# A Mamba scan: the softplus correction shared out between two engines, and a sixth half buffer for the states

## The chip, the cores and the metric

The kernel runs on one core of one Trainium2 chip. A core has five engines that work side by side and meet only through semaphores: TensorE (PE in the profile, with its weight loads as PEld), VectorE (DVE), ScalarE (ACT), GpSimd (POOL) and SyncE (SP), which here only starts transfers. Everything is computed in fp32. The metric is the device time of one execution in microseconds (us), from the first to the last instruction of the core.

## What is computed

The network has four layers on an image batch of 2 x 256 x 32 x 32: two Mamba blocks in a row (layer 0), a dilated 7 x 7 convolution attention (layer 1), a linear attention and a mixture of experts (layer 2), a softmax attention and another mixture of experts (layer 3). The change touches layer 0 alone. Cut to what matters, one Mamba block on a sequence `u` of 1024 positions is

```python
xs, res = split(u @ in_w + in_b)                  # 512 channels each
xs = silu(causal_conv4(xs) + conv_b)
dt, Bm, Cm = split(xs @ xproj_w)                  # 16 + 16 + 16
delta = softplus(dt @ dt_w + dt_b)
dA  = exp(delta[..., None] * A)                   # 16 states per channel
dBu = delta[..., None] * Bm[:, :, None, :] * xs[..., None]
# for each position t:  h = dA_t * h + dBu_t ;  y_t = sum over states of h * C_t
y = (ys + xs * Dp) * silu(res)
out = y @ out_w + out_b                           # then layernorm, added to u
```

The softplus is computed as max(z, 0) + log(1 + e), with e = exp(-|z|). When e is small, 1 + e is rounded, so the kernel adds what the rounding lost: e - ((1 + e) - 1). This term is the softplus correction.

## The kernel before: the parts that matter

The 2 x 1024 positions are cut into 4 chunks of 512 per block, so two blocks make 8 chunks, and a tile holds 128 channels on the partitions. There are 4 such groups of channels (NDC) and 16 states (NS). Each chunk has a `front` (projection, convolution, softplus), a `scan` and a `back` (gate, output projection, layernorm). The first front runs alone, with VectorE doing its softplus; the seven others run beside the scan of the chunk before, with GpSimd doing it. A Python generator cuts each part into pieces, and every slot of a scan (16 states x 4 channel groups = 64 slots) takes a piece of what is to run beside it:

```python
before = m.scan(j, before, chain(*done, *(a.front(k) for a, k in ahead), islice(aside, 7)))
done = [m.back(j)]
```

The framework's scheduler then settles the order of the instructions on each engine; that order need not be the order of the source.

The end of `front`, the softplus (L340 to L369; `eng` is GpSimd unless the front runs alone):

```python
for dc in range(NDC):
    # ... ps = dt_w.T @ dt, on TensorE
    nc.scalar.activation(e[:, dc, :], ps, AF.Abs, bias=b)                       # L349
    # ...
        nc.scalar.activation(delta[:, dc, :], ps, AF.Relu, bias=b)              # L353
    yield
parts = [slice(dc, dc + 1) for dc in range(NDC)] if alone else [slice(0, NDC)]
for a in parts:
    nc.scalar.activation(e[:, a, :], e[:, a, :], AF.Exp, scale=-1.0)            # L357
for a in parts:
    nc.scalar.activation(ln[:, a, :], e[:, a, :], AF.Ln, bias=net.one)          # L359
yield
for dc in range(NDC):
    eng.tensor_scalar(du[:, dc, :], e[:, dc, :], 1.0, -1.0, ALU.add, ALU.add)   # L362
    eng.tensor_sub(du[:, dc, :], e[:, dc, :], du[:, dc, :])                     # L363
    yield
    eng.tensor_add(ln[:, dc, :], ln[:, dc, :], du[:, dc, :])                    # L365
    eng.tensor_add(delta[:, dc, :], delta[:, dc, :], ln[:, dc, :])              # L366
    eng.tensor_mul(du[:, dc, :], delta[:, dc, :], xs[:, dc, :])                 # L367
    yield
```

The scan. Per state n: GpSimd makes the input `h` = du * B in two halves of two channel groups each (one tile of 128 x 1024, five such tiles in the ring), ScalarE makes dA = exp(delta * A) into PSUM (three tiles), VectorE scans in place over `h`, TensorE transposes the scanned states of the state before, and VectorE accumulates them, weighted by C, into `ya`:

```python
for n in range(NS):
    # ... b = B of state n, broadcast over the partitions by a transfer (ring of 4)
    for g in range(NDC // G):                                      # two halves
        h = scanp.tile(half, F32, tag="h", ..., bufs=5)
        nc.gpsimd.tensor_mul(h, du[:, g * G : (g + 1) * G, :], ...b...)        # L414
    for dc in range(NDC):                                          # one slot each
        da = self.ps_da.tile([P, TC], F32, tag="da", ...)
        nc.scalar.activation(da, delta[:, dc, :], AF.Exp, scale=...)           # L421
        nc.vector.tensor_tensor_scan(h, da, h, ..., ALU.mult, ALU.add)         # L425
        next(before, None)         # a piece of rest(n - 1): transpose L393, accumulate L402
        if n or dc:
            next(between, None)    # a piece of back(j - 1), front(j + 1), aside
```

Of `back`, the last pieces: the layernorm's output is turned back, scaled into a tile `r` and added to the running sequence `xt` by GpSimd; in the second block the input image `x` is loaded and added too.

```python
r = self.one.tile([P, TC], F32, tag="r", ..., bufs=2)
nc.scalar.activation(r, ps, AF.Identity, scale=..., bias=...)
nc.gpsimd.tensor_add(xt[:, cc, tok], xt[:, cc, tok], r)
if self.x is not None:
    x = self.one.tile([P, TC], F32, tag="x", ..., bufs=2)
    nc.sync.dma_start(x, ...)
    nc.gpsimd.tensor_add(xt[:, cc, tok], xt[:, cc, tok], x)
```

`ln` and the gate of `back` share one buffer (tag "gate", one tile), and `e` shares one with the convolution's input. Beside the scans run also the pieces of `aside`, which prepare the convolution weights of layer 1 (transpose, copy to `w1ts`, multiply, copy out).

Of the kernel before, what the change touches and what calls it, by code (L numbers as in the profile page):

```python
# [9 lines left out]
F32 = mybir.dt.float32  # L10
I32 = mybir.dt.int32
BF16 = mybir.dt.bfloat16
AF = mybir.ActivationFunctionType
ALU = mybir.AluOpType
# [4 lines left out]
P = 128  # L19
# [7 lines left out]
TC = 512  # L27
# [35 lines left out]
class Net:  # L63


    def __init__(self, ctx, tc, cols, rows):
        self.tc, self.nc = tc, tc.nc
        nc = self.nc
        const = ctx.enter_context(tc.tile_pool(name="const", bufs=1))
        self.small = ctx.enter_context(tc.tile_pool(name="small", bufs=4))  # L70
        self.cols = const.tile([P, NCOLS], F32, name="cols_sb")
        nc.scalar.dma_start(self.cols, cols)
        self.rows = const.tile([P, NROWS], F32, name="rows_sb")
        self.rows_dram = rows
        self.ident = const.tile([P, P], F32, name="ident")
        make_identity(nc, self.ident)
        self.eps5 = const.tile([P, 1], F32, name="eps5")
        nc.vector.memset(self.eps5, 1e-5)
        self.eps6 = const.tile([P, 1], F32, name="eps6")
        nc.vector.memset(self.eps6, 1e-6)  # L80
        self.one = const.tile([P, 1], F32, name="one")
        nc.vector.memset(self.one, 1.0)
        self.ones_row = const.tile([1, P], F32, name="ones_row")
        nc.vector.memset(self.ones_row, 1.0)

# [125 lines left out]
class Mamba:  # L211
# [46 lines left out]
    def front(self, j, alone=False):  # L258


        net, nc, m, one, two = self.net, self.net.nc, self.m, self.one, self.two
        eng = nc.vector if alone else nc.gpsimd
# [3 lines left out]
        xs = two.tile([P, NDC, TC], F32, tag="xs", name=f"{m}_xs_{j}")  # L266
# [71 lines left out]
        delta = two.tile([P, NDC, TC], F32, tag="delta", name=f"{m}_delta_{j}")  # L338
        e = one.tile([P, NDC, 3 + TC], F32, tag="pre", name=f"{m}_e_{j}")[:, :, :TC]
        ln = one.tile([P, NDC, TC], F32, tag="gate", name=f"{m}_ln_{j}")  # L340
        du = two.tile([P, NDC, TC], F32, tag="du", name=f"{m}_du_{j}")
# [13 lines left out]
        parts = [slice(dc, dc + 1) for dc in range(NDC)] if alone else [slice(0, NDC)]  # L355
        for a in parts:
            nc.scalar.activation(e[:, a, :], e[:, a, :], AF.Exp, scale=-1.0)  # L357
        for a in parts:
            nc.scalar.activation(ln[:, a, :], e[:, a, :], AF.Ln, bias=net.one)  # L359
        yield  # L360
        for dc in range(NDC):
            eng.tensor_scalar(du[:, dc, :], e[:, dc, :], 1.0, -1.0, ALU.add, ALU.add)  # L362
            eng.tensor_sub(du[:, dc, :], e[:, dc, :], du[:, dc, :])  # L363
            yield
            eng.tensor_add(ln[:, dc, :], ln[:, dc, :], du[:, dc, :])  # L365
            eng.tensor_add(delta[:, dc, :], delta[:, dc, :], ln[:, dc, :])  # L366
            eng.tensor_mul(du[:, dc, :], delta[:, dc, :], xs[:, dc, :])  # L367
            yield
        self.chunks[j] = xs, bd, ct, delta, du  # L369

    def scan(self, j, before, between):

        net, nc, m, scanp = self.net, self.net.nc, self.m, self.scanp
        xs, bd, ct, delta, du = self.chunks[j]
        state, first = self.state, self.first(j)
        ya = self.two.tile([P, TPC, DI], F32, tag="ya", name=f"{m}_ya_{j}")
        self.chunks[j] = xs, ya
        G = 2  # L380
        half = [P, G, TC]

        def keep(n, hs):
            for g, h in enumerate(hs):
                nc.scalar.copy(state[:, n, g * G : (g + 1) * G], h[:, :, TC - 1])

        def rest(n, hs):


            for i in range(TPC):  # L390
                ps = self.ps_ht.tile([P, DI], F32, tag="ht", name=f"{m}_ht_{j}_{n}_{i}")
                for dc in range(NDC):
                    nc.tensor.transpose(  # L393
                        ps[:, dc * P : (dc + 1) * P], hs[dc // G][:, dc % G, i * P : (i + 1) * P],
                        net.ident,
                    )
                yield
                c = ct[:, i, n : n + 1]
                if n == 0:
                    nc.vector.tensor_scalar_mul(ya[:, i, :], ps, c)  # L400
                else:
                    nc.vector.scalar_tensor_tensor(  # L402
                        ya[:, i, :], ps, c, ya[:, i, :], ALU.mult, ALU.add
                    )
                if i == 0 and first:
                    keep(n, hs)

        for n in range(NS):
            b = scanp.tile([P, TC], F32, tag="b", name=f"{m}_b_{j}_{n}", bufs=4)
            nc.sync.dma_start(b, bd[n].partition_broadcast(P))  # L410
            hs = []
            for g in range(NDC // G):
                h = scanp.tile(half, F32, tag="h", name=f"{m}_h_{j}_{n}_{g}", bufs=5)
                nc.gpsimd.tensor_mul(  # L414
                    h, du[:, g * G : (g + 1) * G, :], b.unsqueeze(1).to_broadcast(half)
                )
                hs.append(h)
            for dc in range(NDC):
                da = self.ps_da.tile([P, TC], F32, tag="da", name=f"{m}_da_{j}_{n}_{dc}")
                i = dc * NS + n  # L420
                nc.scalar.activation(  # L421
                    da, delta[:, dc, :], AF.Exp, scale=self.aneg[:, i : i + 1]
                )
                h = hs[dc // G][:, dc % G, :]
                nc.vector.tensor_tensor_scan(  # L425
                    h, da, h, 0.0 if first else state[:, n, dc : dc + 1], ALU.mult, ALU.add
                )


                next(before, None)  # L430
                if n or dc:
                    next(between, None)
            before = chain(before, rest(n, hs))
        for _ in between:
            pass
        return before

    def back(self, j):

        net, nc, m, xt = self.net, self.net.nc, self.m, self.xt  # L440
# [47 lines left out]
        yield  # L488
        for cc in range(NCC):
            ps = net.transposed(self.ps_mm, tiles, cc, "mm")  # L490
            r = self.one.tile([P, TC], F32, tag="r", name=f"{m}_r_{j}_{cc}", bufs=2)
            nc.scalar.activation(
                r, ps, AF.Identity, scale=net.col(f"{m}_ln_w", cc), bias=net.col(f"{m}_ln_b", cc)
            )
            nc.gpsimd.tensor_add(xt[:, cc, tok], xt[:, cc, tok], r)
            if self.x is not None:
                x = self.one.tile([P, TC], F32, tag="x", name=f"{m}_x_{j}_{cc}", bufs=2)
                at = j % (HW // TC) * TC
                nc.sync.dma_start(x, self.x[j // (HW // TC), cc, :, at : at + TC])
                nc.gpsimd.tensor_add(xt[:, cc, tok], xt[:, cc, tok], x)  # L500
            yield
# [45 lines left out]
class Taps:  # L547
# [9 lines left out]
    def make(self, psum, dram):  # L557

        net, nc, pool = self.net, self.net.nc, self.pool
        self.made = [dram.tile([P, 14, NTAP], F32, name=f"taps_{u}") for u in range(7)]  # L560
        for u in range(7):
            w = pool.tile([P, 14, P], F32, tag="w1", name=f"w1_{u}")
            nc.sync.dma_start(w, self.w1[:, u].rearrange("p v c o -> p (v c) o"))
            out = pool.tile([P, 14, NTAP], F32, tag="taps", name=f"taps_sb_{u}", bufs=1)
            for k in range(0, 14, 4):
                n = min(4, 14 - k)
                ps = psum.tile([P, TC], F32, tag="mm", name=f"w1t_{u}_{k}")
                for i in range(n):
                    nc.tensor.transpose(ps[:, i * P : (i + 1) * P], w[:, k + i, :], net.ident)
                wt = pool.tile([P, TC], F32, tag="w1t", name=f"w1ts_{u}_{k}")  # L570
                nc.scalar.copy(wt[:, : n * P], ps[:, : n * P])
                yield
                ps = psum.tile([P, TC], F32, tag="mm", name=f"taps_ps_{u}_{k}")
                for i in range(n):
                    nc.tensor.matmul(
                        ps[:, i * NTAP : (i + 1) * NTAP], lhsT=wt[:, i * P : (i + 1) * P],
                        rhs=self.w2_sb, start=True, stop=True,
                    )
                nc.scalar.copy(  # L579
                    out[:, k : k + n, :],  # L580
                    ps[:, : n * NTAP].rearrange("p (i t) -> p i t", t=NTAP),
                )
                yield
            nc.sync.dma_start(self.made[u], out)
# [836 lines left out]
```

## Time and profile before

| | us |
|---|---|
| time, median of 3 runs | 2627.21 (2624.74 to 2627.4) |
| span of the profiled execution | 2625.0 |
| busy, PE / DVE / ACT / POOL | 2132.4 / 1503.0 / 964.1 / 1076.5 |
| the scans' transposes (layer 0), first to last start | 57 to 1227 |
| GpSimd: input of a half state (L414), 256 times | 601.0 in all |
| GpSimd: the five softplus lines (L362, L363, L365, L366, L367), 28 times each | 53.6, 32.8, 35.1, 35.1, 35.1 |
| VectorE: the scans (L425), 512 times | 320.5 + 304.8 |
| VectorE: the accumulations (L402), 480 times | 342.9 |
| ScalarE: the exponentials of the scan (L421), 512 times | 350.2 |

How to read it: the busy time of an engine is a sum over the whole kernel, and stages with different limits are added up in it, so a share of the span says little; what holds up a stage is seen in the stretches of that stage and in who waits for whom there. A line of the form "DVE m_h L425 <- POOL m_h L414: 140.0, 27, 19.0" says that VectorE, about to run line 425 on tile m_h, stood idle until GpSimd finished line 414, 140.0 us in all, 27 times, 19.0 at the longest. In a timeline the first two figures are the start and the length in us of a run of like instructions, the count comes last, and idle time just before it stands in brackets with what ended it.

### The profile page before, as it was taken

The numbers are of one execution on the slowest core, as the hardware profiler recorded it, in microseconds if no ns is written. First come the engines' busy times: TensorE is split into PE (matmuls) and PEld (weight loads), VectorE is DVE, ScalarE is ACT, GpSimd is POOL, SyncE is SP. The second block draws the span as 40 slices with busy tenths as digits, with TensorE's granted clock in tenths as the row PEclk, the third lists the DMA queues.
The fourth block names the chain that finished last, engine by engine and source line by source line (L and its number), as shares of the span: only waits on it lengthen the run. The fifth ranks groups of instructions, "written<-read, shape, count | busy, mean of one in ns | idle before, by whom it ended". The sixth has DMA issues, their size and how long they took to land. (4 is left out here: it accounts for less than half of the span.)

```text
span 2625.0 us, 24530 instructions
## 1 busy us (share of the span) xinstructions
PE 2132.4 (81%) x8166; PEld 1320.8 (50%) x8166; DVE 1503.0 (57%) x2252; ACT 964.1 (37%) x1608; POOL 1076.5 (41%) x708
## 2 busy tenths in 40 slices
PE   5868677696868778687899789949999599689995
PEld 2535454454545444454454445635665367546663
DVE  6789699796969798798000766652222424522222
ACT  4644556455455546452000234412211323211123
POOL 2675865758586767863000540003233100023331
PEclk8868688786878878686899789969999799889997
DMA  3010111001111111120000010027888300178884
GB/s 143 29 46 29 30 37 54 28 29 48 28 45 41 44 33 41 45 54 7 7 10 1 0 41 1 17 118 243 309 301 283 125 0 17 35 260 314 312 308 172
DMA packets 74909, 241.87 MB, mean 92 GB/s; under 512 B 21944, under 2 KB 34621, under 8 KB 62624
## 3 DMA queue, kind: packets, MB, share of 16 engines
q1 hardware_dynamic: 65216, 219.18, 24.2%
q0 software_dynamic: 9024, 20.74, 2.5%
q8 instruction: 65, 1.06, 0.2%
q10 hardware_dynamic: 544, 0.40, 0.1%
q14 instruction: 60, 0.49, 0.1%
HBM read 222.87 MB, written 21.33 MB: 93 GB/s over the span
## 5 line engine op out<-in xcount | busy, mean ns | idle before, releaser
L414 POOL TENSOR_TENSOR m_h<-m_du,m_b 128x1024 f32<-128x1024 f32 x256 | 601.0, 2371 | 362.4 <-PE m_ht L393 162.0
L393 PE MATMUL m_ht<-ident,m_h 128*128 128x128 f32 x2048 | 418.5, 340 | 253.5 <-DVE m_ya L402 172.1
L393 PEld LDWEIGHTS m_ht<-ident,m_h 128*128 128x128 f32 x2048 | 300.6, 174 | 459.2 <-issue 183.3
L421 ACT ACTIVATE m_da<-m_delta,m_aneg 128x512 f32<-128x512 f32 x512 | 350.2, 690 | 411.2 <-DVE m_h L425 410.0
L425 DVE TENSOR_TENSOR_SCAN m_h<-m_da,m_state,m_h 128x512 f32<-128x512 f32 x256 | 320.5, 1266 | 70.3 <-POOL m_h L414 66.0
L402 DVE SCALAR_TENSOR_TENSOR m_ya<-m_ht,m_ct,m_ya 128x512 f32<-128x512 f32 x480 | 342.9, 727 | 24.6 <-PE m_ht L393 23.3
L425 DVE TENSOR_TENSOR_SCAN m_h<-m_da,m_h 128x512 f32<-128x512 f32 x256 | 304.8, 1207 | 87.1 <-POOL m_h L414 74.0
L1230 PE MATMUL h<-we,xts 128*128 128x512 f32 x752 | 342.4, 598 | 1.0 <-DVE xts L1220 1.0
L1202 POOL DMA_INDIRECT x<-l_zd,source x94 | 95.9, 1020 | 512.7 <-DVE source L1166 448.3
L1237 DVE TENSOR_TENSOR hid<-hid,h 128x512 f32<-128x512 f32 x94 | 64.7, 688 | 292.6 <-PE h L1230 273.1
L1261 POOL DMA_INDIRECT yd<-y,target x94 | 95.7, 1018 | 328.0 <-DMA yd<-y,target 182.7
L1230 PEld LDWEIGHTS h<-we,xts 128*128 128x128 f32 x752 | 137.3, 193 | 138.9 <-issue 137.1
L1255 PE MATMUL o<-we,hts 128*128 128x256 f32 x752 | 179.3, 382 | 1.5 <-ACT hts L1248 1.5
L1248 ACT COPY hts<-ht 128x512 f32<-128x512 f32 x94 | 55.1, 586 | 337.5 <-PE ht L1244 337.5
L651 PE MATMUL acc<-act,pair 128*98 128x448 f32 (+14 forms) x448 | 165.2, 517 | 0.0
L1255 PEld LDWEIGHTS o<-we,hts 128*128 128x128 f32 x752 | 136.3, 191 | 17.9 <-ACT hts L1248 1.9
L1260 DVE COPY y<-o 128x256 f32<-128x256 f32 x94 | 39.9, 425 | 131.2 <-PE o L1255 66.1
L301 PE MATMUL m_conv<-m_pre,m_taps 128*128 128x512 f32 x240 | 112.5, 592 | 0.0
L447 PE MATMUL m_g<-act,m_gate_sb 128*128 128x512 f32 x128 | 80.0, 715 | 35.9 <-ACT taps_sb L579 35.9
L651 PEld LDWEIGHTS acc<-act,pair 128*98 128x98 f32 x448 | 73.5, 166 | 70.0 <-issue 53.8
L1236 ACT ACTIVATE hid<-h 128x512 f32<-128x512 f32 x94 | 56.1, 597 | 99.0 <-PE h L1230 98.9
L666 DVE COPY lg<-acct 98x512 f32<-98x512 f32 x1 | 0.7, 691 | 139.5 <-PE acct L657 139.5
(295 smaller groups left out, 3097.7 us busy)
## 6 DMA issues: line engine op xcount, KB each, us to landing
we<-in_l_experts_dram SPq DMA_DIRECT2D x94, 1536.0 KB, 8.3
m_b<-m_bd SPq DMA_DIRECT2D x128, 256.0 KB, 3.1
yl<-yd SPq DMA_DIRECT2D x16, 512.0 KB, 5.0
w<-in_l_w_dram SPq DMA_DIRECT2D x7, 896.0 KB, 5.8
l_zd<-l_z SPq DMA_DIRECT2D x8, 512.0 KB, 2.9
taps<-taps_sb SPq DMA_DIRECT2D x7, 343.0 KB, 3.6
pair<-taps SPq DMA_DIRECT2D x7, 343.0 KB, 4.0
act<-in_x_dram SPq DMA_DIRECT2D x4, 512.0 KB, 5.1
```

What stands on the lines that cost most here:

```text
L301: nc.tensor.matmul(ps, lhsT=self.taps[:, dc * 4 + k, :], rhs=pre[:, dc, k : k + TC], start=(k == 0), stop=(k == 3),)
L393: nc.tensor.transpose(ps[:, dc * P : (dc + 1) * P], hs[dc // G][:, dc % G, i * P : (i + 1) * P], net.ident,)
L402: nc.vector.scalar_tensor_tensor(ya[:, i, :], ps, c, ya[:, i, :], ALU.mult, ALU.add)
L414: nc.gpsimd.tensor_mul(h, du[:, g * G : (g + 1) * G, :], b.unsqueeze(1).to_broadcast(half))
L421: nc.scalar.activation(da, delta[:, dc, :], AF.Exp, scale=self.aneg[:, i : i + 1])
L425: nc.vector.tensor_tensor_scan(h, da, h, 0.0 if first else state[:, n, dc : dc + 1], ALU.mult, ALU.add)
L447: nc.tensor.matmul(ps, lhsT=self.gate_sb[:, kc, dc * P : (dc + 1) * P], rhs=xt[:, kc, tok], start=(kc == 0), stop=(kc == NCC - 1),)
L651: nc.tensor.matmul(acc[b, k][:, lo - 16 * k : hi - 16 * k, co : co + n], lhsT=lhsT, rhs=x4[:, kc, b, lo - r0 : hi - r0, ci : ci + n], star ...
L1202: nc.gpsimd.indirect_dma_start(out=x, out_offset=None, in_=zd[:, :], in_offset=bass.IndirectOffsetOnAxis(ap=source[:, g : g + 1], axis=0), ...
L1230: nc.tensor.matmul(ps, lhsT=xt[:, kc * P : (kc + 1) * P], rhs=w12[:, s, kc, :], start=(kc == 0), stop=(kc == NCC - 1),)
L1255: nc.tensor.matmul(ps[:, :C], lhsT=ht[:, mc * P : (mc + 1) * P], rhs=w[:, 8 + mc, :], start=(mc == 0), stop=(mc == NHC - 1),)
L1261: nc.gpsimd.indirect_dma_start(out=yd[:, :], out_offset=bass.IndirectOffsetOnAxis(ap=target[:, g : g + 1], axis=0), in_=y, in_offset=None, ...
```

## The change

It does four things. It takes (1 + e) - 1 off GpSimd, in the fronts that run beside a scan, and gives it to ScalarE as two Identity activations; the subtraction, the two additions and the product stay on GpSimd. It spreads the softplus over more pieces: one operation or two to a slot, four slots for a channel group and 16 in all in place of 8, and Exp and Ln in different slots. It gives the inputs of the states a sixth half buffer, so that GpSimd may be half a state further ahead of the scan. And it pays for that buffer by letting r and x share a ring of three tiles and by keeping one `w1ts` tile instead of two. The aim is that GpSimd's softplus does not hold up the inputs of the scan.

```diff
+        self.minus_one = const.tile([P, 1], F32, name="minus_one")
+        nc.vector.memset(self.minus_one, -1.0)
 ...
         for a in parts:
             nc.scalar.activation(e[:, a, :], e[:, a, :], AF.Exp, scale=-1.0)
+        yield
         for a in parts:
             nc.scalar.activation(ln[:, a, :], e[:, a, :], AF.Ln, bias=net.one)
         yield
         for dc in range(NDC):
-            eng.tensor_scalar(du[:, dc, :], e[:, dc, :], 1.0, -1.0, ALU.add, ALU.add)
-            eng.tensor_sub(du[:, dc, :], e[:, dc, :], du[:, dc, :])
+            w = du[:, dc, :]
+            if alone:
+                nc.vector.tensor_scalar(w, e[:, dc, :], 1.0, -1.0, ALU.add, ALU.add)
+            else:
+                nc.scalar.activation(w, e[:, dc, :], AF.Identity, bias=net.one)
+                nc.scalar.activation(w, w, AF.Identity, bias=net.minus_one)
+            eng.tensor_sub(w, e[:, dc, :], w)
             yield
-            eng.tensor_add(ln[:, dc, :], ln[:, dc, :], du[:, dc, :])
+            eng.tensor_add(ln[:, dc, :], ln[:, dc, :], w)
+            yield
             eng.tensor_add(delta[:, dc, :], delta[:, dc, :], ln[:, dc, :])
-            eng.tensor_mul(du[:, dc, :], delta[:, dc, :], xs[:, dc, :])
+            yield
+            eng.tensor_mul(w, delta[:, dc, :], xs[:, dc, :])
             yield
 ...
-                h = scanp.tile(half, F32, tag="h", name=f"{m}_h_{j}_{n}_{g}", bufs=5)
+                h = scanp.tile(half, F32, tag="h", name=f"{m}_h_{j}_{n}_{g}", bufs=6)
 ...
-            r = self.one.tile([P, TC], F32, tag="r", name=f"{m}_r_{j}_{cc}", bufs=2)
+            r = self.one.tile([P, TC], F32, tag="r", name=f"{m}_r_{j}_{cc}", bufs=3)
 ...
-                x = self.one.tile([P, TC], F32, tag="x", name=f"{m}_x_{j}_{cc}", bufs=2)
+                x = self.one.tile([P, TC], F32, tag="r", name=f"{m}_x_{j}_{cc}", bufs=3)
 ...
-                wt = pool.tile([P, TC], F32, tag="w1t", name=f"w1ts_{u}_{k}")
+                wt = pool.tile([P, TC], F32, tag="w1t", name=f"w1ts_{u}_{k}", bufs=1)
```

## The prediction

> **What bounds the kernel now.** I read the page first, then a table of stretches, then VectorE's waits, then the timelines of GpSimd and VectorE around its longest waits.
>
> The page says that no engine is at its limit on average (PE 81%, DVE 57%, POOL 41%), so the limit has to be read by stage. The change touches only the Mamba layer, which by the first and last state transposes runs from 57 to 1227 us. Its stretches of 80 us:
>
> ```profile
> core 0: us, PE busy (x) PEld busy (x) DVE busy (x) ACT busy (x) POOL busy (x), PEclk, DMA share, GB/s
> 160.00:240.00 80.00, 58.66 (x251) 38.74 (x251) 80.00 (x100) 37.71 (x60) 49.97 (x22) 0.71 0.12 34
> 240.00:320.00 80.00, 63.22 (x238) 38.86 (x236) 57.41 (x62) 44.74 (x63) 56.92 (x35) 0.76 0.09 28
> ...
> 880.00:960.00 80.00, 51.00 (x218) 34.33 (x216) 58.98 (x66) 42.82 (x63) 64.71 (x38) 0.70 0.13 45
> 960.00:1040.00 80.00, 71.36 (x292) 43.75 (x293) 73.30 (x93) 45.21 (x79) 47.18 (x24) 0.89 0.12 38
> ```
>
> The reader sees VectorE (third figure) at 80.00 of 80 where GpSimd has only scan inputs to make, and at 57 to 59 where GpSimd (fifth) is busiest. So this stage is VectorE's, with holes. From 57 to 1230 us VectorE is busy 990 us of 1173. Who makes the holes:
>
> ```profile
> engine line waited for: us in total, times, longest us
> DVE m_h L425 <- POOL m_h L414: 140.0, 27, 19.0
> DVE m_ya L402 <- PE m_ht L393: 23.3, 26, 1.8
> DVE m_h L425 <- ACT m_da L421: 17.4, 9, 4.0
> DVE m_xs L468 <- PE m_y L464: 0.9, 1, 0.9
> ```
>
> Their sum, 181.6, is the whole idle time. Line by line in VectorE's timeline, seven waits on GpSimd stand out, one per `front` that runs beside a scan: 15.3, 19.0, 14.6, 19.0, 15.4, 19.0 and 15.3 us, four of them followed by 0.55: 119.8 us. The other 20 are pairs of 1.5 and 1.2 us near states 5 and 6. The 19.0 of the second scan, seen on GpSimd:
>
> ```profile
> 290.48 4.69 POOL L414 TENSOR_TENSOR m_h<-m_du,m_b 128x1024 f32<-128x1024 f32 x2 [1.26 <-DVE m_ya L402]
> 295.13 3.82 POOL L362 TENSOR_SCALAR m_du<-m_e 128x512 f32<-128x512 f32 x2
> 298.91 2.33 POOL L363 TENSOR_TENSOR m_du<-m_e,m_du 128x512 f32<-128x512 f32 x2
> ...
> 319.45 2.49 POOL L367 TENSOR_TENSOR m_du<-m_delta,m_xs 128x512 f32<-128x512 f32 x2
> 321.89 9.29 POOL L414 TENSOR_TENSOR m_h<-m_du,m_b 128x1024 f32<-128x1024 f32 x4
> ```
>
> All twenty softplus instructions stand in one block between two inputs of the scan, 295.13 to 321.89 = 26.8 us; VectorE needs the next input at 305.3 and gets it at 324.3.
>
> **What the Trainium skill says.** "GPSIMD Engine Reference", section 3.1, gives 4497 ns for a two-input fp32 op of 2048 elements, about 1.96 times VectorE. The trace agrees in kind: 1270 ns for 512 against 684 on VectorE. Its 4.1 calls one-input ops about line-rate; here the trace disagrees, the one-input L362 takes 1931 ns, more than a two-input add, and the measurement decides: this op is the right one to take off GpSimd. "ScalarE: Activation LUTs", Rules for kernel authors, budgets about 0.3 us and 0.83 ns an element, 0.73 us for 512; the trace has 0.62 for an Exp of that size between SBUF tiles, which I use. "TensorE: Matmul & The Clock Gate", Part 1, says that the array is throttled by default and activity releases it; the stretches agree (0.70 to 0.76 with the holes, mostly 0.81 to 0.89 without), so filled holes should not cost TensorE clock.
>
> **The change part by part.**
>
> *GpSimd's work.* Removed: 28 L362 x 1.931 = 54 us. Left per front: 4 x (1.18 + 3 x 1.25) = 20 us instead of 27.
>
> *Where it stands.* I compared the two kernels' order of instructions on each engine. (s = the subtraction, a and d the two adds, u the product, 13.1 = second half of state 13.) Before, even scans (counted from 0) have 19 of the 20 softplus operations in one block, odd scans all 20. Afterwards even: `12.1 [s a d u s a] 13.0 [d] 13.1 [u s a d u] 14.0 14.1 [s a d u] 15.0`; odd: `13.1 [s s a a d d u u s a d] 14.0 [u] 14.1 [s a d u] 15.0`.
>
> *The sixth half buffer.* A scan slot takes 1.77 to 1.83 us in the undisturbed timeline (one scan and one accumulation), so a state takes 7.2 and a half 3.6. State n's inputs may be written once the transposes of an earlier state have read the tile. In the undisturbed timeline these end about 4.8 us into the following state (GpSimd restarts at 160.42, that state's scans began at 155.6 to 156.2). With six halves 13.0 and 13.1 start when state 10 is transposed, 4.8 us after its end, and finish 4.7 later; state 14 is needed 3 x 7.2 = 21.5 after its end. Lead on entering the block: 21.5 - 9.5 = 12 us. Before, the blocks were entered with 8 to 10 (a wait of ScalarE set aside).
>
> *The stalls left.* One op 1.24, one half input 2.33; each half earns 3.6 us of lead.
> Odd: 11 ops 13.5 + 2.33 = 15.8 against 12: stall 3.8. Then [u] + 14.1 = 3.6 against 3.6: nothing. Then 4 ops + 15.0 = 7.3 against 3.6: 3.7. Sum 7.5 instead of 19.0.
> Even: 6 ops + input 9.6 against 12: lead 2.4 left. [d] + 13.1: still 2.4. 5 ops + 14.0 = 8.5 against 2.4 + 3.6: stall 2.5. 14.1 earns 1.3; 7.3 against 4.9: 2.4. Sum 4.9 instead of about 15.7.
> Total 4 x 4.9 + 3 x 7.5 = 42 us where 119.8 stood.
>
> *The short pairs near states 5 and 6*, 20 us: there GpSimd itself waits for TensorE (10.7 us idle before m_h), because a buffer is missing while TensorE does the gate and projection matmuls. A half buffer more should cover half: 10 us left.
>
> *ScalarE.* Added: 56 Identity x 0.62 = 35 us, 5 us a front. On average there is room (617 us busy of 1173). What matters is the clump around Ln, table load 1.28 + Ln 2.0 + table load 1.28, in which no m_da is made, while VectorE has three PSUM tiles ahead (5.4 us). In odd scans all four first Identity operations stand inside this clump, before the next m_da: +2.5 us; in even scans one, +0.6, and one after the next m_da. The waits on m_da were 4.0 (even) and 1.4 (odd) and 0 in one scan; I expect 4.8 and 3.9: 4 x 4.8 + 3 x 3.9 = 31 us instead of 17. Exp and Ln in separate slots do not change the number of table loads (98 in both orders).
>
> *TensorE.* Same instructions. 23 us of waits stay.
>
> *r, x, w1t.* x now shares a ring of three with r, so it is loaded in the same scan instead of a scan ahead, once GpSimd has got through state 6, and the second x after r's add. Both sit under the 12 us lead there. At the end of the layer it may add 1 us. w1t with one buffer: its matmuls already stood between two of its copies. Nothing.
>
> *Sum.* VectorE idle after: 42 + 10 + 31 + 23 + 1 = 107, plus 1 at the end = 108, instead of 182. Gain 74 us; the later layers (1240 us on) stay. 2627 - 74 = about 2552 us.
>
> **The rivals.**
> 1. *The holes vanish.* If a front of 20 us spread over 16 slots (29 us) hides wholly and ScalarE's additions too, all 140 us of the GpSimd waits go: about 2490. For: spread evenly, a slot would cost GpSimd 1.17 us of inputs and 1.24 of softplus, 2.4 against 1.8, and over 16 slots a lead of 12 us pays for the difference of 10. Against: the order on GpSimd bunches the work into fewer slots than the source asks for.
> 2. *ScalarE takes over.* Its Identity operations stand in line before m_da, and gate's first activation now waits for GpSimd's last add into the shared tile. If each front loses 8 to 10 us to ScalarE rather than 4.4, +30 us: about 2580. For: the clump at Ln grows by 2.5 in odd scans. Against: elsewhere there is at most one Identity between two m_da, about 1.3 us in a 1.8 us slot.
> 3. *The sixth buffer gives no lead*, because TensorE transposes late. With a lead of 8.4: odd 7.4 + 3.7, even 1.2 + 4.9 + 2.4, total 67 instead of 42: about 2577.
> 4. *TensorE becomes the bound.* It is busy 886 us of 1173 at clock 0.77. If filled holes only push it into waiting, half the gain goes: about 2590. Against: 80.00 of 80 on VectorE with the clock at 0.71.
>
> **Range and chances.** The removal of the long waits is nearly sure; the sizes of what replaces them are not: 15 us for the lead, 15 for ScalarE, 10 for the short pairs, together about 22. 8 in 10: 2526 to 2580. The 2% line is 2575; rivals 2 to 4 must come together in part to cross it: 0.84 faster, 0.15 within, 0.01 slower, as nothing adds work to VectorE, the limiting engine of the stage.
>
> **What would show it.** Right: VectorE's wait on m_h from GpSimd falls from 140 to about 50, none over 6 us; its wait on m_da rises to about 30; its wait on m_ht stays near 23; the last transposes start near 1153 instead of 1227; GpSimd loses some 54 us of busy time and ScalarE gains 35. Wrong: single waits on m_h of 8 us and more (no lead), m_da waits above 50 (ScalarE), m_ht waits above 50 (TensorE), or a difference after the Mamba layer.

## The result, and the profile after

| | before | after |
|---|---|---|
| time, median of 4 runs each | 2625.97 us (2623.7 to 2627.4) | 2541.5 us (2540.18 to 2549.33) |
| ratio, 95% interval | | 0.9685 (0.9664 to 0.9707) |
| span of the profiled execution | 2625.0 | 2538.9 |
| last transposes of the scans start at | 1226.7 | 1147.2 |
| VectorE's waits within the scans, their sum | 181.6 | 94.1 |

The kernel is faster by 84 us, 3.2%. 2552 was predicted, with 2526 to 2580 around it.

The first line is from the page of after: busy time of each engine. The second group is its table of stretches, to be read beside that of before (the fields are those of the header).

```profile
PE 2098.9 (83%) x8166; PEld 1303.4 (51%) x8166; DVE 1507.6 (59%) x2253; ACT 998.8 (39%) x1664; POOL 1025.1 (40%) x680
```

```profile
core 0: us, PE busy (x) PEld busy (x) DVE busy (x) ACT busy (x) POOL busy (x), PEclk, DMA share, GB/s
57.00:1145.00 1088.00, 851.66 (x3557) 541.95 (x3558) 991.19 (x1163) 651.44 (x1019) 757.23 (x396) 0.80 0.14 41
160.00:240.00 80.00, 61.23 (x257) 39.80 (x256) 80.00 (x99) 41.03 (x64) 48.45 (x23) 0.77 0.13 38
240.00:320.00 80.00, 60.49 (x245) 39.57 (x243) 64.57 (x71) 48.41 (x70) 61.45 (x35) 0.74 0.12 35
```

GpSimd lost 51.4 us of busy time and ScalarE gained 34.7; VectorE's work in the layer is nearly what it was: up to its last accumulation it is busy 994 us in place of 988, for 1167 instructions both times, but they now take 1091 us instead of 1170.5. The stretch from 240 us still has a hole: 64.57 of 80 where it was 57.41. The layer ends 79.5 us earlier. The remaining 6.6 us of the two profiled spans lie behind the layer and are not shown to be the change's: a second execution of the changed kernel (the last experiment) has 1397 us there and before has 1398, where this one has 1392, and the kernels below have 1387 to 1400.

VectorE's waits within the layer, after (in total, times, longest):

```profile
DVE m_ya L412 <- PE m_ht L403: 34.2, 24, 4.9
DVE m_h L435 <- ACT m_da L431: 28.5, 9, 4.6
DVE m_h L435 <- POOL m_h L424: 25.7, 19, 2.8
DVE m_h L435 <- ACT m_state L395: 4.9, 2, 4.7
```

Of these L424 is the input of the states (L414 of before), L431 the dA, L435 the scan, L403 and L412 the transposes and accumulations. The wait on GpSimd, which was 140.0 us with 19.0 at the longest, is down to 25.7 with 2.8. The long holes are gone, and there is less left of them than the prediction's 52. But two lines went up: TensorE from 23.3 to 34.2, ScalarE from 17.4 to 28.5, and a third is new (4.9).

The block in the second scan, which had held VectorE up for 19.0 us; GpSimd's timeline of after, and then VectorE's (start, length, count last, idle before in brackets):

```profile
282.42 4.65 POOL L424 TENSOR_TENSOR m_h<-m_du,m_b 128x1024 f32<-128x1024 f32 x2 [0.25 <-PE m_ht L403]
287.03 2.32 POOL L371 TENSOR_TENSOR m_du<-m_e,m_du 128x512 f32<-128x512 f32 x2
...
299.19 1.27 POOL L375 TENSOR_TENSOR m_delta<-m_delta,m_ln 128x512 f32<-128x512 f32 x1
300.42 2.36 POOL L424 TENSOR_TENSOR m_h<-m_du,m_b 128x1024 f32<-128x1024 f32 x1
302.73 1.28 POOL L377 TENSOR_TENSOR m_du<-m_delta,m_xs 128x512 f32<-128x512 f32 x1
303.95 2.36 POOL L424 TENSOR_TENSOR m_h<-m_du,m_b 128x1024 f32<-128x1024 f32 x1
```

```profile
279.07 1.27 DVE L435 TENSOR_TENSOR_SCAN m_h<-m_da,m_state,m_h 128x512 f32<-128x512 f32 x1
281.04 2.73 DVE L412 SCALAR_TENSOR_TENSOR m_ya<-m_ht,m_ct,m_ya 128x512 f32<-128x512 f32 x4 [0.70 <-PE m_ht L403]
286.37 5.98 DVE L435 TENSOR_TENSOR_SCAN m_h<-m_da,m_state,m_h 128x512 f32<-128x512 f32 x5 [2.60 <-ACT m_da L431]
...
305.08 1.27 DVE L435 TENSOR_TENSOR_SCAN m_h<-m_da,m_state,m_h 128x512 f32<-128x512 f32 x1
306.27 0.73 DVE L412 SCALAR_TENSOR_TENSOR m_ya<-m_ht,m_ct,m_ya 128x512 f32<-128x512 f32 x1
311.56 1.28 DVE L435 TENSOR_TENSOR_SCAN m_h<-m_da,m_state,m_h 128x512 f32<-128x512 f32 x1 [4.56 <-ACT m_da L431]
```

The block is as predicted, eleven operations and then the first half of state 14, 287.03 to 302.78: 15.75 us, where 15.8 was worked out. What was wrong is the lead. VectorE scans this half only from 305.08, 18.05 us after GpSimd entered the block, and not 12. So the block costs nothing. The 6 us more are seen in the same lines: state 10's last scan ended at 280.34 and its tile was free at 282.42, 2.1 us later instead of 4.8 (2.7 us gained), and VectorE then stood 0.70 + 2.60 us itself, for TensorE and for ScalarE, before it went on. 12 + 2.7 + 3.3 = 18.0.

The last line shows something else that nobody asked for: 4.56 us of waiting for dA, far from the clump around Ln. ScalarE's waits in the layer have a line that before has not:

```profile
ACT taps_sb L589 <- DMA taps<-taps_sb: 31.8, 5, 8.1
```

and in ScalarE's timeline it stands just ahead of that 4.56:

```profile
302.40 0.59 ACT L581 COPY w1ts<-w1t 128x512 f32<-128x512 f32 x1 [0.82 <-PE w1t L579]
310.61 0.32 ACT L589 COPY taps_sb<-taps_ps 128x196 f32<-128x196 f32 x1 [7.62 <-DMA taps<-taps_sb]
310.82 0.70 ACT L431 ACTIVATE m_da<-m_delta,m_aneg 128x512 f32<-128x512 f32 x1
```

This belongs to `aside`, the weights of layer 1. There is one `taps_sb` tile; its contents are stored to memory, and the next copy into it (L589) has to wait for the store. The next dA (L431) stands behind that copy on ScalarE and starts at 310.82. Why the store is late is on SyncE's queue, first of after, then of before:

```profile
255.85 50.80 SPq L420 DMA_DIRECT2D m_b<-m_bd  x7
306.70 0.42 SPq L594 DMA_DIRECT2D taps<-taps_sb  x1
```

```profile
263.13 30.07 SPq L410 DMA_DIRECT2D m_b<-m_bd  x5
298.12 0.32 SPq L584 DMA_DIRECT2D taps<-taps_sb  x1
324.27 18.10 SPq L410 DMA_DIRECT2D m_b<-m_bd  x4
```

The last of the seven loads of B in after was issued at 306.33, just as GpSimd finished the second half of state 14 (303.95 + 2.36 = 306.31), whose B it overwrites. The store behind it was issued at 306.70, though its data were there since 298.1 (ScalarE's copy at 297.85 took 0.23). In before's order the store comes ahead of such loads, and it was SyncE that waited for the data. The front now takes more slots, so the pieces of `aside` behind it come later in the scan, and the store fell behind the loads of the next scan. It lands about 4 us later, and VectorE pays 4.56 here. Four such places can be told in VectorE's timeline, in four of the seven scans: 4.56 (dA), 4.94 (transposes, TensorE being held up by its turn of the same tiles), 3.03 (dA) and 4.75 (the `m_state` above): 17.3 us.

### The profile page after: what moved, and what is told of

It is laid out like the page before. It is cut to its first block, busy times and chain, and to the rows that moved or that the text cites. A ratio compares the mean times of both kernels' runs of the same rounds, so it can differ in the third digit from the quotient of the medians.

```text
span 2538.9 us, 24630 instructions
## 1 busy us (share of the span) xinstructions
PE 2098.9 (83%) x8166; PEld 1303.4 (51%) x8166; DVE 1507.6 (59%) x2253; ACT 998.8 (39%) x1664; POOL 1025.1 (40%) x680
## 3 DMA queue, kind: packets, MB, share of 16 engines
q1 hardware_dynamic: 65216, 219.18, 25.3%
## 5 line engine op out<-in xcount | busy, mean ns | idle before, releaser
L424 POOL TENSOR_TENSOR m_h<-m_du,m_b 128x1024 f32<-128x1024 f32 x256 | 600.9, 2372 | 307.3 <-PE m_ht L403 113.8
L403 PE MATMUL m_ht<-ident,m_h 128*128 128x128 f32 x2048 | 412.9, 336 | 209.8 <-DVE m_ya L412 114.7
L403 PEld LDWEIGHTS m_ht<-ident,m_h 128*128 128x128 f32 x2048 | 297.3, 171 | 403.5 <-issue 152.2
L431 ACT ACTIVATE m_da<-m_delta,m_aneg 128x512 f32<-128x512 f32 x512 | 350.2, 689 | 273.3 <-DVE m_h L435 272.4
L412 DVE SCALAR_TENSOR_TENSOR m_ya<-m_ht,m_ct,m_ya 128x512 f32<-128x512 f32 x480 | 342.4, 728 | 36.4 <-PE m_ht L403 34.2
L435 DVE TENSOR_TENSOR_SCAN m_h<-m_da,m_state,m_h 128x512 f32<-128x512 f32 x256 | 320.1, 1267 | 24.7 <-ACT m_da L431 14.6
L435 DVE TENSOR_TENSOR_SCAN m_h<-m_da,m_h 128x512 f32<-128x512 f32 x256 | 303.9, 1206 | 34.7 <-POOL m_h L424 15.7
L1265 PEld LDWEIGHTS o<-we,hts 128*128 128x128 f32 x752 | 136.7, 192 | 17.9 <-ACT hts L1258 1.9
L457 PE MATMUL m_g<-act,m_gate_sb 128*128 128x512 f32 x128 | 73.6, 664 | 17.4 <-ACT taps_sb L589 12.9
```

The lines of the kernel that those rows point to most:

```text
L403: nc.tensor.transpose(ps[:, dc * P : (dc + 1) * P], hs[dc // G][:, dc % G, i * P : (i + 1) * P], net.ident,)
L412: nc.vector.scalar_tensor_tensor(ya[:, i, :], ps, c, ya[:, i, :], ALU.mult, ALU.add)
L424: nc.gpsimd.tensor_mul(h, du[:, g * G : (g + 1) * G, :], b.unsqueeze(1).to_broadcast(half))
L431: nc.scalar.activation(da, delta[:, dc, :], AF.Exp, scale=self.aneg[:, i : i + 1])
L435: nc.vector.tensor_tensor_scan(h, da, h, 0.0 if first else state[:, n, dc : dc + 1], ALU.mult, ALU.add)
L457: nc.tensor.matmul(ps, lhsT=self.gate_sb[:, kc, dc * P : (dc + 1) * P], rhs=xt[:, kc, tok], start=(kc == 0), stop=(kc == NCC - 1),)
```

## The experiments

Two questions. First, which of the three parts (ScalarE, the spreading, the sixth half) brings what, and is the lead really what makes the sixth half worth it? Second, is the late store a cost of the change that can be taken away? The first seven kernels are the changed one with parts undone, in all combinations; r and x keep their shared ring and `w1ts` its one tile throughout. All of them compute the same thing.

| ScalarE | spread | sixth half | time, us | ratio to before (95%) | VectorE waits for GpSimd / ScalarE's dA / TensorE's transposes | last transposes |
|---|---|---|---|---|---|---|
| - | - | - | 2625.71 | 1.0002 (0.9987 to 1.0017) | 139.2 / 16.3 / 26.6 | 1228.9 |
| - | - | yes | 2592.71 | 0.9888 (0.9849 to 0.9926) | 109.3 / 14.6 / 17.8 | 1193.1 |
| - | yes | - | 2604.45 | 0.9913 (0.9896 to 0.9929) | 119.7 / 16.4 / 23.4 | 1208.8 |
| yes | - | - | 2559.2 | 0.9747 (0.973 to 0.9763) | 48.6 / 36.6 / 25.3 (put right below) | 1163.8 |
| yes | - | yes | 2524.59 | 0.9617 (0.9583 to 0.9652) | 19.2 / 37.0 / 23.0 | 1134.5 |
| yes | yes | - | 2559.88 | 0.9753 (0.9718 to 0.9787) | 59.2 / 24.7 / 28.1 | 1161.1 |
| - | yes | yes | 2584.43 | 0.9831 (0.9795 to 0.9868) | 70.8 / 36.0 / 26.9 | 1186.2 |
| yes | yes | yes (after) | 2541.5 | 0.9685 (0.9664 to 0.9707) | 25.7 / 28.5 / 34.2 | 1147.2 |

**Nothing but the ring.** All three parts undone.

```diff
-        yield                                   # between Exp and Ln
-                nc.scalar.activation(w, e[:, dc, :], AF.Identity, bias=net.one)
-                nc.scalar.activation(w, w, AF.Identity, bias=net.minus_one)
+            eng.tensor_scalar(w, e[:, dc, :], 1.0, -1.0, ALU.add, ALU.add)
-            yield                               # after the first and the second add
-                h = scanp.tile(half, F32, tag="h", ..., bufs=6)
+                h = scanp.tile(half, F32, tag="h", ..., bufs=5)
```

> The payback alone: r and x share three tiles, w1ts has one tile, the softplus stands as before (one GpSimd operation for (1+e)-1, eight slots) and h has five halves. My theory: the blocks on GpSimd are those of before, so the time is that of before, within 5 us of 2626. A rival that the shared ring or the single w1ts tile costs or gains something by itself would show 10 us or more either way.

Measured: 2625.71 beside 2626.04. What the sixth buffer is paid with costs nothing that shows, as the prediction had it.

**The sixth half alone.** The same, but with six.

```diff
-                nc.scalar.activation(w, ...Identity...)   # and the extra slots
+            eng.tensor_scalar(w, e[:, dc, :], 1.0, -1.0, ALU.add, ALU.add)
                 h = scanp.tile(half, F32, tag="h", ..., bufs=6)
```

> Only the sixth half buffer (with the payback). My theory (block plus one input minus lead): the block of twenty operations, 28 us with its input, still stands whole, and the lead grows from about 8.4 to 12, 3.6 us a front and a little less where the block begins half a state later: 17 to 21 us less than before in all, about 2607. The rival that the buffer is what does it (GpSimd was short of tiles, not of time) expects 60 us less or more, below 2570. The rival that only work taken off GpSimd counts expects no change, 2626.

Measured: 2592.71, 33 us off where about 19 had been expected. VectorE's and ScalarE's waits:

```profile
DVE m_h L428 <- POOL m_h L417: 109.3, 19, 15.2
DVE m_ya L405 <- PE m_ht L396: 17.8, 12, 4.5
...
ACT m_gate L454 <- POOL m_delta L369: 61.1, 7, 10.4
```

The seven long waits became 12.7, 15.2, 11.5, 15.0, 12.7, 14.8 and 12.7, each some 2.5 to 4 us shorter, about one half state of lead (3.6) each: 23 us in all, which the expectation had nearly right. What it did not count is that the other waits for GpSimd fell by 7 and those for the transposes by 9 us beside the kernel with nothing but the ring. The ACT line is new: the gate's tile, which it shares with `ln`, is released by GpSimd's last add, and ScalarE stands for it. No cost of it is seen on VectorE, whose waits for dA are 14.6 us beside 16.3.

**The spreading alone.** Five halves, (1 + e) - 1 on GpSimd, but in 16 slots.

```diff
+            eng.tensor_scalar(w, e[:, dc, :], 1.0, -1.0, ALU.add, ALU.add)
             eng.tensor_sub(w, e[:, dc, :], w)
             yield                               # the extra slots stay
-                h = scanp.tile(half, F32, tag="h", ..., bufs=6)
+                h = scanp.tile(half, F32, tag="h", ..., bufs=5)
```

> Only the spreading over 16 slots (with the payback); GpSimd still does (1+e)-1 and h has five halves. My theory: the order on GpSimd breaks the block of twenty into pieces of seven to fifteen operations, but its total stays 27 us a front, so the pieces' stalls add up to nearly what the block cost: by the rule about 21 us less than before in all, about 2605. A rival that spreading is the heart of the change expects 50 us less or more.

Measured: 2604.45, as expected. A long hole is cut into several (36 waits instead of 27, the longest 10.5), and their sum falls by only 20 us: the work of the block is all still GpSimd's.

**ScalarE alone.** Five halves, eight slots, (1 + e) - 1 on ScalarE.

```diff
                 nc.scalar.activation(w, e[:, dc, :], AF.Identity, bias=net.one)
                 nc.scalar.activation(w, w, AF.Identity, bias=net.minus_one)
-            yield                               # the extra slots
-                h = scanp.tile(half, F32, tag="h", ..., bufs=6)
+                h = scanp.tile(half, F32, tag="h", ..., bufs=5)
```

> Only the handing of (1+e)-1 to ScalarE (with the payback); eight slots, five halves. My theory: each block loses four operations of 1.93 us and begins later, by the rule 59 us less waiting on GpSimd in all, less 14 us more waiting on m_da around Ln: 45 us less than before, about 2581. The rival that GpSimd's work is all that counts expects 54 us less here and nothing from the other two parts. The rival that the buffer or the spreading does it expects 20 us less at most.

Measured: 2559.2. This was 22 us better than expected. GpSimd gave up four operations of 1.93 us a front, 7.7 us, or 54 us in seven fronts. The waits, and an odd scan's (GpSimd's timeline, then VectorE's):

```profile
DVE m_h L432 <- POOL m_h L421: 59.8, 25, 5.6
DVE m_h L432 <- ACT m_da L428: 25.3, 12, 7.1
```

```profile
282.54 9.31 POOL L421 TENSOR_TENSOR m_h<-m_du,m_b 128x1024 f32<-128x1024 f32 x4 [1.25 <-DVE m_ya L409]
291.94 1.28 DVE L432 TENSOR_TENSOR_SCAN m_h<-m_da,m_state,m_h 128x512 f32<-128x512 f32 x1 [3.97 <-POOL m_h L421]
```

The line for GpSimd has too much in it. The scan at 291.94 is the first of state 11, whose input had been there for 10.65 us; the four inputs that GpSimd finishes at 291.85 are later ones. What came just before the scan is its dA, at 291.83. The same holds for 3.93 and 3.36 in the two other odd scans. So 11.3 us are ScalarE's: 48.6 for GpSimd, 91 less than with nothing but the ring, and 36.6 for dA, 20 more. (In the other kernels no such wait of a scan is put down to the wrong engine.)

The wait of 7.09 for dA lies in three of the even scans, where five of the eight Identity operations stand in the clump between Ln and the table load behind it, and is followed by 4.26 for GpSimd. Added, 11.35, they are about what the prediction's rule gives for the block alone: 17.0 for the unbroken block (measured in the next kernel) + 2.4 for the input - 8.4, the lead with five halves, = 11.0. In the odd scan a wait of 4.22 for GpSimd follows the 3.97 in the same way. The two engines keep VectorE waiting at the same place, so what one takes the other does not take again. Whether this makes up all of the 22 us was not worked out.

**ScalarE and the sixth half, no spreading.**

```diff
         for a in parts:
             nc.scalar.activation(e[:, a, :], e[:, a, :], AF.Exp, scale=-1.0)
-        yield
 ...
             eng.tensor_add(ln[:, dc, :], ln[:, dc, :], w)
-            yield
             eng.tensor_add(delta[:, dc, :], delta[:, dc, :], ln[:, dc, :])
-            yield
             eng.tensor_mul(w, delta[:, dc, :], xs[:, dc, :])
```

> The changed kernel with the softplus back in eight slots (Exp and Ln in one slot); ScalarE's share and the sixth half stay. My theory: the block on GpSimd is whole again (13 to 16 operations), and by the rule of block, input and lead 17 us of waits more: about 2558. The rival that spreading is worth its 22 us of the single experiment expects 2563; the rival that it is worth nothing once ScalarE has its share expects 2541, and less than that if the stretched front is what makes ScalarE wait for the transfer of the convolution weights (32 us of ScalarE's waits in the changed kernel, none before).

Measured: 2524.59 (2521.81 to 2530.24), 17 us faster than the changed kernel and with an interval that does not meet its. The expectation of 2558 counted the whole block against a lead of 12 us. VectorE's waits, then GpSimd's timeline in the first scan, then VectorE's there:

```profile
DVE m_h L432 <- ACT m_da L428: 37.0, 14, 7.1
DVE m_ya L409 <- PE m_ht L400: 23.0, 18, 2.5
DVE m_h L432 <- POOL m_h L421: 19.2, 17, 1.5
```

```profile
114.05 4.67 POOL L421 TENSOR_TENSOR m_h<-m_du,m_b 128x1024 f32<-128x1024 f32 x2 [2.10 <-issue]
120.29 1.26 POOL L370 TENSOR_TENSOR m_du<-m_e,m_du 128x512 f32<-128x512 f32 x1 [1.57 <-ACT m_du L369]
...
136.11 1.27 POOL L372 TENSOR_TENSOR m_ln<-m_ln,m_du 128x512 f32<-128x512 f32 x1
137.33 2.37 POOL L421 TENSOR_TENSOR m_h<-m_du,m_b 128x1024 f32<-128x1024 f32 x1
```

```profile
103.39 2.33 DVE L432 TENSOR_TENSOR_SCAN m_h<-m_da,m_h 128x512 f32<-128x512 f32 x2
...
115.16 1.22 DVE L432 TENSOR_TENSOR_SCAN m_h<-m_da,m_h 128x512 f32<-128x512 f32 x1
123.47 2.51 DVE L432 TENSOR_TENSOR_SCAN m_h<-m_da,m_h 128x512 f32<-128x512 f32 x2 [7.09 <-ACT m_da L428]
...
139.73 1.23 DVE L432 TENSOR_TENSOR_SCAN m_h<-m_da,m_h 128x512 f32<-128x512 f32 x1 [0.49 <-POOL m_h L421]
```

The block stands unbroken from 120.29 to 137.3 and holds VectorE up by 0.49 us. VectorE needs the input at 139.24, 18.95 us after the block was entered. That is about 12 for the buffers and 7.09 for its own wait, but the parts are others. VectorE takes 33.5 us from the end of state 5's last scan (105.72) to 139.24, 12 more than three undisturbed states, with the 7.09 and 1.92 for the transposes among them. Against that GpSimd began the inputs that take over state 5's tiles only 8.3 us after that end, not 4.8, and then stood 1.57 us for ScalarE. Spreading has next to nothing to remove here: the waits for GpSimd are 1.5 us at the longest in the whole layer. And there is no wait for the store: in this order SyncE reaches the store first.

**No sixth half, and no ScalarE.** The two remaining combinations.

```diff
-                h = scanp.tile(half, F32, tag="h", ..., bufs=6)
+                h = scanp.tile(half, F32, tag="h", ..., bufs=5)
```

> The changed kernel with five halves; ScalarE's share and the spreading stay. My theory: 3.6 us of lead less in each of seven fronts: 15 to 25 us more, 2556 to 2566. The rival that the sixth half keeps its 33 us of the single experiment expects 2574; the rival that it is needless after the other two parts expects 2541.

```diff
-                nc.scalar.activation(w, e[:, dc, :], AF.Identity, bias=net.one)
-                nc.scalar.activation(w, w, AF.Identity, bias=net.minus_one)
+            eng.tensor_scalar(w, e[:, dc, :], 1.0, -1.0, ALU.add, ALU.add)
```

> The changed kernel with (1+e)-1 back on GpSimd; spreading and the sixth half stay. My theory: 27 us of operations a front against 29 us of slots plus inputs, by the rule 60 us more waits on GpSimd, less 14 on ScalarE around Ln: about 2585. If the gains of the single experiments simply add (33 + 22), 2571.

Measured: 2559.88 and 2584.43, both as expected. With the table full, the spreading can be read off four times: 21 us gained when it is alone, about 8 with the sixth half (the two intervals overlap), nothing measurable with ScalarE, and 17 lost when both are there. The three parts gain 33 + 22 + 67 = 122 us singly, against before, and 84 together. They work on the same blocks, and the spreading is there for a block that the other two have already hidden. ScalarE waits for the store in all four kernels with the spreading (17.0, 11.3, 16.6 and 31.8 us) and in none of the four without, so the late store comes with the spreading.

**The store from ScalarE's queue.** The changed kernel with one line changed, so that the store does not stand behind the loads of B.

```diff
-            nc.sync.dma_start(self.made[u], out)
+            nc.scalar.dma_start(self.made[u], out)
```

> The changed kernel with one line more: the finished convolution weights are stored from ScalarE's queue instead of SyncE's, where the store stands behind three loads of the next scan's b. My theory: ScalarE's 32 us of waits for that transfer go, and with them waits of VectorE of 5 to 7 us in each of four or five scans; GpSimd takes back a part: 8 to 20 us less than the changed kernel, 2522 to 2533. Rival: GpSimd's wait is only uncovered, VectorE waits for m_h instead, and the time stays at 2541 within 3.

Measured: 2524.27 (2517.15 to 2528.86), ratio 0.9618 (0.9584 to 0.9651), as expected. The waits of VectorE, and the store's own record (its durations, first and last start):

```profile
DVE m_h L435 <- POOL m_h L424: 34.5, 24, 2.8
DVE m_ya L412 <- PE m_ht L403: 22.5, 15, 4.5
DVE m_h L435 <- ACT m_da L431: 20.8, 6, 4.6
...
L594 ACTq DMA_DIRECT2D taps<-taps_sb x7: 344/344/345, 301.0 to 1051.1; - x7
```

No wait of ScalarE for the store is left. TensorE's transposes are back at 22.5 and dA at 20.8; GpSimd's rises by 9, since VectorE, held up less, comes to the inputs sooner. The last transposes start at 1128.3, 19 us earlier (in the execution profiled, the fastest of the four). So the late store, and not the spreading as such, made the changed kernel slower than the one without the spreading: moved, it takes the whole 17 us away.

**Eight slots and the store from ScalarE's queue.** Both of the last gains in one.

```diff
-            yield                               # the extra slots
-            nc.sync.dma_start(self.made[u], out)
+            nc.scalar.dma_start(self.made[u], out)
```

> Softplus in eight slots, ScalarE's share, six halves, and the store of the convolution weights on ScalarE's queue. My theory: the store cost time only where ScalarE waited for it, which in the eight-slot kernel it never did, so the two gains of 17 us are one and the same and do not add: 2524 within 4. Rival: moving the store helps by itself (SyncE's queue freed) or the eight slots do, and the two add: about 2508.

Measured: 2531.56 (2523.74 to 2538.46) beside 2626.93 for before on its chip, ratio 0.9626 (0.9596 to 0.9656). They do not add: without the spreading the store was not late, so there was nothing left to gain. It came out 7.6 us above the expected 2524, outside the 4 allowed for; the interval meets those of the two kernels at 2524, so no loss is shown either. The same chip has the changed kernel at 2543.15, though these two intervals touch as well.

**VectorE takes (1 + e) - 1.** Eight slots, six halves, but the operation that left GpSimd goes to VectorE in all fronts, one instruction of 0.42 us instead of two Identity.

```diff
-            yield                               # the extra slots
-            if alone:
+            if True:
                 nc.vector.tensor_scalar(w, e[:, dc, :], 1.0, -1.0, ALU.add, ALU.add)
```

> Eight slots and six halves, but (1+e)-1 on VectorE instead of ScalarE. My theory: VectorE gets 28 x 0.42 = 12 us more to do, and its waits on m_da around Ln fall from 37 to about 20 us: near balance, 2515 to 2527. Rival, from the skill's page on SBUF (a VectorE operation with one SBUF source in its two-port form and a GpSimd operation block each other): the operation takes well over 0.42 us beside GpSimd, or GpSimd's operations lengthen, 2535 or more.

Measured: 2546.77, ratio 0.969 (0.9662 to 0.9719), 22 us worse than with ScalarE; the rival came true. The operation in this kernel, and in before, where it ran on VectorE only in the front that runs alone (durations shortest, median, longest in ns):

```profile
L366 DVE TENSOR_SCALAR m_du<-m_e x32: 395/1310/2585, 40.9 to 990.9; 128x512 f32<-128x512 f32 x32
```

```profile
L362 DVE TENSOR_SCALAR m_du<-m_e x4: 416/420/427, 40.0 to 50.3; 128x512 f32<-128x512 f32 x4
```

Of the 32, the four that run alone are among the short ones; with the 28 beside GpSimd's block the median is 1310 ns instead of 420. The Trainium skill, "SBUF — State Buffer", section "Who interferes with whom", says that VectorE's second port pair is shared with GpSimd under an exclusive lock; the spread of durations agrees with a wait for it. The 28 of them take 41.4 us, on the engine that sets the stage, in place of about 12. Some of it is offset: the scans' waits for dA, 37.0 us with ScalarE, are gone from its list; those for GpSimd are 42.8 in place of 19.2.

**Four tiles for dA, two for the transposes.** Eight slots, six halves; ScalarE's clump was to be bridged by a fourth PSUM tile.

```diff
-            yield                               # the extra slots
-        tc.tile_pool(name="m_da", bufs=3, space=PSUM) as ps_da,
-        tc.tile_pool(name="m_ht", bufs=3, space=PSUM) as ps_ht,
+        tc.tile_pool(name="m_da", bufs=4, space=PSUM) as ps_da,
+        tc.tile_pool(name="m_ht", bufs=2, space=PSUM) as ps_ht,
```

> Eight slots, ScalarE's share and six halves; of the eight PSUM banks the exponentials get four instead of three and the transposes two instead of three. My theory: the waits around Ln are a matter of how many m_da VectorE has ahead; one more is worth 1.8 us in each of seven fronts: 10 to 13 us less than the eight-slot kernel, about 2513. Rival: the transposes need the third bank, VectorE's waits on m_ht grow from 23 to 50 us or more: 2545 or more.

Measured: 2572.29, ratio 0.9789 (0.9755 to 0.9822), 48 us worse than with three and three; here too the rival came true. VectorE's waits up to 1150 us, 36 us before this layer's end:

```profile
DVE m_ya L409 <- PE m_ht L400: 62.3, 59, 4.5
DVE m_h L432 <- POOL m_h L421: 53.6, 21, 6.0
DVE m_h L432 <- ACT m_da L428: 17.3, 6, 3.4
```

The fourth tile does what it should: the wait at the clump falls from 7.1 to 3.4 in the three even scans that had it. But the third transpose tile is worth more: TensorE's wait rises from 23.0 to 62.3, in 59 pieces (63.7 to the layer's end), and GpSimd's from 19.2 to 53.6, presumably because a half buffer comes free only when the transposes have read it.

**The changed kernel again.** Unaltered, beside the last three.

> The changed kernel itself beside the others on one chip. If the spreading really costs time once the other two parts are in, it stays at 2541 within 5, some 17 us above the eight-slot kernel. If the 17 us were a difference of chips, it comes out near 2525.

Measured: 2543.15 (2536.67 to 2552.18), ratio 0.9675 (0.9642 to 0.9707); ScalarE's wait for the store 31.4 us, the last transposes at 1153.2. The late store is there in both executions profiled.

## Why the prediction was right, point by point

The mechanism was right: GpSimd's long blocks were the holes, and what was to fill them did. The number, 74 us for 84, is right in part by luck: the terms of the sum were off by up to 33 us, in both directions.

**The bound.** Right. The stage is VectorE's, with holes made by GpSimd's blocks; filling them shortened the layer by about what they lost. TensorE, rival 4, did not become the bound: the granted clock in the layer rose from 0.77 to 0.80. The clock does not follow VectorE's holes closely, though: from 400 to 480 us it is 0.68 with VectorE busy 73.0 of 80, where before it was 0.72 with 59.0.

**What goes and what comes.** GpSimd's 54 us: 51.4. ScalarE's 35 us: 34.7 of busy time. The single Identity takes 0.706 us at the mean, not 0.62; two in a row overlap by some 0.09 (1.32 for a pair), so the sum came out right for a reason that was not in it. The trace of before had the nearer model: Ln of the same size, which takes its bias from a tile as Identity does, took 704 ns there.

**The blocks: 42 us predicted, 9.5 measured.** This is the term that was furthest off: 0.42 and 2.71, 2.79, 0.43, 0.42 and 2.72 are all that is left. The operations' order and their sum were right (15.75 us for 15.8). The lead of 12 us was too small: it is about 18 in the odd scan shown, since the transposes caught up and VectorE's own waits are lead for GpSimd. The prediction had set the waits for ScalarE beside those for GpSimd and added them; they lie at the same place and are paid once. The kernel without spreading shows it best, with 18.95 us of lead and a block of 17 us that costs 0.49. The late store hides a part too: with it moved, the blocks cost 17.9. There each even scan has 0.4 and 2.7 where 2.5 and 2.4 were worked out, and the odd ones have one wait of 1.2 to 2.8 where 3.8 and 3.7 were: it is the first stall, the one behind the lead, that was too large.

**The short pairs: 10 predicted, 16 measured.** Half a state more of buffer did little for them (20 before). GpSimd waits there for TensorE, and why a half more buffer does not bridge it was not tried.

**dA: 31 predicted, 28.5 measured.** Right in sum by luck: the clumps gave 20.6 (4.64 in three even scans, nothing in the fourth; 2.60, 2.88 and 1.24 in the odd), and 7.6 came from the late store.

**TensorE: 23 predicted, 34.2 measured, and "w1t: nothing".** The single `w1ts` tile costs nothing, as the first experiment has it, but the prediction looked at the matmuls of `aside` and not at where its store stands on SyncE's queue. The store costs VectorE 17.3 us directly (4.94 of them in the 34.2), and with it moved the kernel is 17 us faster. Two more waits, 4.49 and 4.48 in the last two of the seven scans, come while TensorE does the front's products for delta (`m_dt`); with the store moved there is one like them, and the changed kernel run again has three, so they are not the store's, and what decides them was not tried. So the ledger closed at 94 against 107 because 33 us too much for the blocks and 10 for the clumps stood against 17 too little for the store, 6 for the pairs and 6 for the other transposes.

**The rivals.** Rival 1 (the holes vanish) was nearer for the blocks than the prediction itself, but it has ScalarE's waits vanish too, and those grew. Rival 2's new wait exists: the gate for GpSimd's last add is 8.4 us in the changed kernel, and 83.1 us where GpSimd keeps (1 + e) - 1; with ScalarE doing its share it stays small. Rival 3 (no lead from the sixth buffer) is refuted: the sixth half gains 33 us alone, 35 on top of ScalarE and 18 on top of both others.

**The spreading.** The prediction gave it credit for cutting the blocks. With the sixth half and ScalarE there, it gains nothing, and it made the store late. Of the kernels measured, the changed one without the spreading (2524.59) and the changed one with the store moved (2524.27) are the fastest, and no difference between them is shown.

## What to carry to other kernels

A buffer's lead is to be worked out from where the consumer will stand, its own other waits included: two engines that hold up the same consumer at the same place are paid once, here about the longer of the two. When work is spread over more slots, look at everything that is pushed later by it, stores too: a transfer that stands behind another which waits for a semaphore waits with it, and a one-tile buffer turns that into a wait of a compute engine. And when several measures aim at one hole, try them without each other; here the third one was worth 21 us alone and cost 17 beside the other two.

## What was not expected of the hardware

With VectorE's one-input operation beside them, GpSimd's adds and multiplies keep their durations (1.27 us, and 2.37 for the state inputs, in every kernel here) and its subtraction goes from 1182 to 1271 ns at the median, while VectorE's operation goes from 420 to 1310 ns, 2585 at the longest. Nearly the whole price of the encounter is VectorE's. And a transfer of 343 KB whose data were ready at 298.1 us was issued at 306.7, right behind a load that stood ahead of it in SyncE's queue and was issued at 306.33; from ScalarE's queue no such delay was left.
